# Weight quantization shared with ScalarE, the causal mask on GpSimd in every batch, and a new instruction order, in a one-core transformer layer

## The chip, the cores and the metric

The kernel runs on one core of a Trainium2 chip. Its metric is the device time of one execution, in microseconds (us); below it is the median over several runs. The engines are named as in the profile: PE (TensorE: matmuls and transposes, PEld its weight loads), DVE (VectorE), ACT (ScalarE), POOL (GpSimd) and SP (SyncE, which here only issues DMAs).

## The reference

Four batches of 512 tokens by 512 channels, float32. A layer has two halves, each preceded by the same kind of gate:

```
gate(x, s, w, u):  # per channel, scans over the tokens in both directions
    ek = exp(min(s, 30));  ekv = ek * s;  euk = exp(min(u + s, 30))
    num = scan_forward(ekv) + scan_backward(ekv) - ekv + euk * s
    den = scan_forward(ek)  + scan_backward(ek)  - ek  + euk
    return sigmoid(x) * num / max(den, 1e-8) * (0.8 + 0.2 * tf)
x = x + attention(gate(x, side, w1, u1))      # 16 heads of 32, causal softmax
h = gate(x, side, w2, u2)
x = x + q_act(silu(q_act(h) @ q_w(w_gate).T) * (q_act(h) @ q_w(w_up).T)) @ q_w(w_down).T
```

The last matrices are 2048 by 512 (gate, up) and 512 by 2048 (down). `q_w` and `q_act` quantize blocks of 32 values along the contracted axis: a block is divided by a power of two taken from its largest magnitude, each value is rounded half to even to a tiny float format and clipped (weights: one fraction bit, at most 6), and multiplied by the power of two again.

## The kernel before

Everything is planned at build time. The code first registers each small piece of work with `add(engine, cost, run, r, w, ...)`, which derives the dependences from the tiles read and written and numbers the operations. Then `Plan.follow` walks through `SEQUENCE`, a list of these numbers that a search found offline against the costs given to `add`, and the instructions are issued in that order; on each engine they run in exactly that order. The costs only serve this planning (PSUM banks are also assigned by it).

DVE instructions marked `shared=True` and POOL instructions are planned to take turns: a POOL instruction gets a dependence on the last shared DVE instruction ahead of it in the list, so it waits for it.

The stages, by batch `b`:

- **Gate** (`wkv_pieces`, lines 602 to 718). Per batch and block of 128 channels: the side input is loaded and transposed (L615), exponentials on ACT (L619 to L634), products on POOL (L626, L652, L654, L665), two forward and two backward scans on DVE (L640, L645) with a scaling on ACT between them (L650), a reciprocal by logarithm and exponential on ACT (L658, L659, L661), and the ratio on DVE (L666, L670, L672, L675). The first gate also transposes x (L689, L692), the second writes its result to DRAM (L709, L712).
- **Attention** (`Group`, four groups of four heads per batch). Projections (L765 for queries and keys, with ACT copies L776 and L779; L731 for values). `find_max`: scores by PE with a mask added by matmuls (L790, L794), row maxima on DVE (L804). `lay_max`: these maxima are split and transposed into `low` (ACT L816, DVE L817, PE L821, ACT L824). `weights`, the score turn: in three turns per group, scores by key (PE L848 subtracts the maxima, L855 adds the products), exponential on ACT (L862) into `pT`. `weigh`: `pT` times the values and times ones (L887, ACT L897). `finish`: the sums are spread and their reciprocals applied (L910, L915, L922, L926). The output projection is L983, its residual L989; the second gate's sigmoid L992 and product L993 follow.
- **Causal mask of the weights.** Two of the three score turns of a group hold diagonal blocks, two each. In batches 0 and 1 (`LATE = 2`) four matmuls (L844) write the mask into the PSUM tile `scores` before the products are added. In batches 2 and 3 two POOL selects (L867) set the upper part of the diagonal blocks of `pT` to zero after the exponential.
- **Weights of the second half** (`weight_piece`, `quantize_weight`). 24 pieces of 128 by 1024, each loaded by SP, quantized and transposed by DMA into `wgT`, `wuT` and `wdT`. They are registered with batch 0 and spread by the list over the first 478 us. Per piece: block maxima (L489), scale and its inverse (L492, L495), division (L513), clip (L515), exponent bits as 16-bit integers (L518), then a factor that turns them into a magic number (L521), all on DVE; POOL adds the magic number (L523), subtracts it (L524), and multiplies by the scale (L525).
- **Second half** (`inner_piece`, `down_piece`). Per tile of 128 tokens: gate and up matmuls (L1020), SiLU on ACT (L1027), product on DVE (L1030), quantization (DVE L489 to L537, POOL L544), DMA transpose, down matmuls (L1061), residual (L1074). Those of batch `b` run beside the attention of later batches. The very last tile is transposed by PE (L555, L1037).

ACT needs a table set loaded for exponential and logarithm, sigmoid, or SiLU. Operations that need one name it in `add`, and a load (L1145) is issued wherever the set changes in the list.

Of the kernel before, what the change touches and what calls it, by code (L numbers as in the profile page):

```python
# [24 lines left out]
ROUND_W, LEAST_W, LIMIT_W = 1.5 * 2.0**22, 0.25, 1.5  # L25
# [116 lines left out]
BEGIN = 3.0  # L142
# [6 lines left out]
0 1 183 30 6 919 27 245 196 33 31 28 2 3 4 29 9 32 34 45 39 40 66 184 185 186 5 187 11 188 16 35 12 10 189 13 14  # L149
41 7 67 937 72 78 42 43 68 46 73 17 47 8 44 15 197 79 105 106 198 50 18 199 19 23 51 74 80 48 49 81 82 111 112  # L150
55 56 107 113 117 36 37 52 190 246 89 20 21 22 38 191 53 54 83 57 58 62 192 94 144 69 118 70 90 95 87 24 25 26
88 119 91 145 120 121 96 200 71 146 59 150 75 84 85 60 86 92 122 93 61 133 201 202 128 97 76 213 108 160 151 277
152 129 156 109 126 127 134 110 77 98 99 203 63 64 101 100 130 193 65 247 114 131 132 115 123 147 161 278 116
279 280 281 248 135 102 194 195 402 262 157 148 124 149 137 125 138 103 104 139 136 204 282 249 250 290 285 140
214 168 164 205 215 217 216 286 291 283 206 218 207 208 343 153 141 142 143 263 264 287 265 221 158 165 169 162
166 170 159 163 167 171 219 292 220 284 222 174 172 173 175 223 226 260 261 227 288 289 266 228 224 225 403 230
404 180 344 231 345 181 182 209 346 405 239 251 240 267 210 241 211 229 347 232 242 406 349 350 243 176 348 293
233 234 351 294 212 408 352 252 268 235 356 353 410 295 244 177 296 357 258 259 236 297 407 253 354 237 360 355
254 275 276 303 309 466 154 155 467 592 238 304 358 269 298 411 305 306 307 361 362 299 359 363 364 365 412 310
255 311 415 308 300 301 468 409 322 323 470 270 366 369 477 469 367 475 416 413 478 370 371 476 428 178 179 419  # L160
420 398 414 471 271 272 479 429 430 482 483 421 431 480 481 312 417 418 484 399 337 486 422 338 257 256 302 324
368 472 473 474 339 432 423 424 340 487 425 488 426 485 489 400 535 313 533 433 536 447 490 314 491 537 540 534
401 541 538 449 273 274 544 450 372 427 586 920 539 587 715 448 493 492 494 542 341 342 325 495 588 589 496 590
545 326 327 543 546 497 591 498 464 465 595 547 315 597 598 548 549 602 599 328 716 512 513 593 550 553 551 596
603 552 709 584 600 554 555 329 594 717 613 614 316 330 604 615 606 616 582 607 601 605 609 653 608 658 583 610
317 527 654 528 651 652 585 529 617 611 659 655 530 531 612 373 532 660 618 632 633 318 656 662 657 710 663 664
711 712 713 319 661 714 718 671 665 672 331 332 333 374 375 720 634 673 719 674 675 721 676 666 725 722 667 767
649 689 668 726 635 690 736 727 772 737 738 763 703 723 724 728 732 334 669 729 730 768 731 773 785 765 766 733
734 769 770 776 786 735 376 764 825 321 320 385 670 819 771 787 788 704 650 820 777 821 823 822 336 335 377 386
434 963 705 378 387 830 706 774 789 790 803 824 775 831 778 826 827 707 804 846 828 379 847 779 708 780 781 832  # L170
835 380 848 849 850 829 851 817 782 783 836 818 964 864 865 878 381 833 839 840 841 435 837 388 891 389 834 838
892 884 879 965 880 842 382 843 844 845 390 391 392 906 436 437 881 886 438 887 907 885 893 888 904 905 393 394
395 784 957 384 383 451 396 397 499 882 916 908 439 889 890 894 452 453 917 918 883 951 952 440 441 454 953 958
933 455 909 954 934 959 895 896 897 960 961 921 442 443 444 955 935 500 968 922 456 898 457 458 962 501 899 900
973 969 956 984 924 925 926 927 910 459 936 966 967 974 911 460 928 929 985 1004 930 502 1005 446 445 923 461
970 931 971 1101 514 1143 938 990 462 463 932 556 986 1006 901 1007 987 902 1008 1009 939 988 1024 914 515 516
517 503 504 505 506 975 940 507 942 972 943 976 1025 1052 1028 1033 518 944 945 946 947 557 1029 989 977 915 978
979 1026 912 992 980 948 1054 1053 981 949 508 509 1085 1034 913 1027 982 1086 1030 983 1031 1035 993 558 559
1068 1087 1032 1036 1037 1038 1039 1088 1046 1047 1069 519 520 521 1040 1041 1042 1089 1090 903 941 1010 1095
991 950 511 510 569 522 1048 1096 1102 1097 1099 523 1091 1049 570 560 1106 1092 995 1103 1098 1107 524 996 1104  # L180
1137 1100 1012 1043 571 572 1138 1013 561 1108 1044 1105 1070 1139 1140 1050 1141 1109 1071 1115 1093 997 998
999 1000 1116 1117 1142 1001 562 563 1051 1111 1112 1002 1094 1122 1147 1123 1148 1224 526 525 1011 994 619 1045
1423 1014 1218 1003 1225 573 574 575 1113 1162 620 1157 1110 1114 564 1118 1175 1176 1177 1149 1155 1163 1015
1441 1016 1158 1226 1195 1119 576 1196 1120 1191 1192 1150 1197 1151 1198 1156 1152 1159 1199 1200 1153 1214
1017 1018 1019 1121 1154 1164 1215 565 577 1160 1161 1166 1219 1193 566 1165 1167 1168 1220 1221 1222 1251 1227
1223 578 1194 621 1229 1252 1253 1254 1230 1228 1169 1170 1171 1234 1231 1245 1172 1173 1235 622 1020 1236 623
1280 1285 1255 1256 1257 1216 1232 1238 1233 1237 1241 1424 1334 567 568 636 1174 1328 579 580 581 1239 1240
1258 1278 1246 1281 1279 1242 1243 1282 1217 1286 1272 1298 1283 1289 1290 1273 1244 637 638 1284 1329 1274 677
1469 1291 1330 1332 639 1287 1288 1299 1300 1021 1316 1331 1301 1317 624 625 626 1275 1302 1318 1337 1319 1338
1339 1292 1333 1470 1335 1340 627 628 1320 1321 1293 1341 1344 1326 1294 1295 1336 1276 1327 629 1342 1022 1343  # L190
1471 1345 1348 1296 1357 1346 1347 1351 1349 1358 1277 1359 1360 1361 640 1380 641 642 643 644 645 646 631 630
1297 1023 691 1463 648 647 739 1355 1350 1362 1376 1352 1353 1354 1378 1356 1379 1381 1410 1408 1377 1411 1409
678 679 680 681 1382 682 683 684 685 686 692 693 694 1385 695 696 697 1398 1386 1399 698 1420 1400 1421 1401 687
1383 1384 1422 740 1439 1455 1456 741 742 1387 1440 1389 1402 1403 699 1388 700 688 751 1464 1457 1437 743 1438
1412 1465 1467 1458 1390 1391 1459 1466 1472 1413 1460 1425 1392 744 745 746 1474 1393 752 1426 1490 1414 1394
1491 1475 1428 1510 1511 1512 1415 1513 1473 701 1468 747 1429 748 1461 749 753 1430 1431 754 1476 1479 1536
1492 1395 1514 1477 1493 1396 1480 1483 1484 1485 1515 1611 702 1427 791 792 1432 793 1481 1541 1443 1444 1442
1496 1397 750 1445 805 1462 1478 1482 1534 1494 1530 1542 1535 1537 1418 1486 755 1433 794 756 757 1434 758 1531
1560 1495 1419 1435 1532 1416 1533 759 1417 1487 1488 1489 1538 1561 1562 1539 1540 1576 795 1543 1577 1605 1436
1446 1593 1545 1447 1594 1448 1554 1595 1606 1555 1596 1544 1607 1608 1609 1556 1612 1597 1498 1598 1601 1449  # L200
1450 796 1451 1452 797 798 1557 806 1616 1499 1546 1614 1547 1617 1453 1610 1516 1497 1738 1518 1621 1548 1549
1550 760 761 1599 1600 799 1454 1500 762 1613 1501 1602 1618 1551 1622 1615 1647 1552 807 1648 1519 808 1623
1578 1649 1558 1650 1619 1579 1625 1651 1502 1620 1626 1624 1628 800 1943 852 1517 1553 1732 1674 1627 1675 1559
853 1669 1629 809 810 811 1630 1603 1652 1667 1670 1604 1657 1632 1739 1658 1740 1668 1687 1659 1660 801 1661
1631 1671 1689 1688 1676 1707 1708 854 855 856 1672 1673 1703 1633 1678 1662 1709 1733 1663 1710 1734 1735 1679
1677 1704 1736 857 812 858 1743 1711 1705 1680 1741 1712 1744 1681 1682 1683 813 1713 1737 1728 1684 1745 1706
1742 1746 1730 1664 1729 1748 1685 1752 1753 1765 1754 1731 1766 814 815 1714 1747 1796 1665 1767 1768 1749 1797
1666 1750 1769 1770 1759 1751 1771 1760 1794 1772 1520 802 1852 866 1686 1846 816 1503 867 1801 1802 1795 1055
1056 1755 859 1756 1757 1798 1758 1814 1853 1816 1057 1815 860 1799 1800 1773 1774 1847 1817 1854 1832 1848 1504
1833 868 1803 1818 1834 1788 1849 1850 1857 1835 1805 1806 1807 1836 1837 1858 861 1851 1804 1862 1808 1809 1810  # L210
# [43 lines left out]
def adaln_attn_ffn(  # L254
# [16 lines left out]
    nc = tc.nc  # L271
# [941 lines left out]
```

## Time and profile before

| | |
|---|---|
| time, median of 3 runs | 762.88 us (762.46 to 764.87) |
| profiled execution | 767.15 us, span 765.4 us |
| instructions | 14324 |
| mean granted PE clock | 0.971 of full |
| ACT table loads, L1145 | 74, 1.283 us each |
| DMA | 68.57 MB, mean 90 GB/s |

The span reaches from the first to the last instruction; the rest of the execution lies around it. In the profile a group of instructions is a line of the kernel with engine, operation, tiles and shape; its columns are the total busy time in us, the mean of one in ns, and the idle time of the engine just before them with what ended it. A "stretch" gives busy us of each engine between two times, with the number of instructions in brackets, then the granted PE clock, the share of DMA and GB/s.

### The profile page before, as it was taken

How to read it: one execution, taken by the hardware profiler on the slowest of the kernel's cores; microseconds unless marked ns; L12 is line 12 of the kernel's file. 1: busy time of each engine (PE TensorE's matmuls, PEld its weight loads, DVE VectorE, ACT ScalarE, POOL GpSimd, SP SyncE). 2: the span in 40 equal slices, each digit the busy share in tenths (PEclk: the TensorE clock that was granted, in tenths of full speed). 3: DMA queues.
4: the chain of work that ended last, by engine and by line, in shares of the span. 5: the costliest groups of instructions: out<-in, count | busy, mean ns of one | idle time of the engine just before them, and what ended most of it. 6: DMA issues, size and time to landing. Idle time of an engine off the chain costs nothing.

```text
span 765.4 us, 14324 instructions
## 1 busy us (share of the span) xinstructions
PE 679.4 (89%) x5636; PEld 356.0 (47%) x5666; DVE 639.3 (84%) x881; ACT 485.1 (63%) x687; POOL 428.0 (56%) x316
## 2 busy tenths in 40 slices
PE   3578889877999988599998869999999999999995
PEld 2344445444444554354554444544444455444442
DVE  5888899998999999999999987766565669789996
ACT  5998798769466878636688877634541566433421
POOL 1976683867778587778686875332231223334440
PEclk9688999989999999999999999999999999999999
DMA  7553152131345523325343100233313225446542
GB/s 220 152 138 82 30 132 63 43 98 41 83 125 127 148 53 98 86 72 138 90 118 112 42 16 8 69 63 76 97 36 84 56 42 100 100 94 164 103 104 82
DMA packets 115730, 68.57 MB, mean 90 GB/s; under 512 B 71632, under 2 KB 98256, under 8 KB 115664
## 3 DMA queue, kind: packets, MB, share of 16 engines
q1 hardware_dynamic: 115664, 67.67, 34.9%
q8 instruction: 44, 0.72, 0.4%
q14 instruction: 22, 0.18, 0.1%
HBM read 38.81 MB, written 12.58 MB: 67 GB/s over the span
## 4 chain that ended last, share of the span: by engine, by line
PE 65%; DVE 16%; ACT 10%; issue 4%; DMA 3%; POOL 2%; SPq 0%; DVEq 0%; POOLq 0%; ACTq 0%
PE bank L1020 13%; PE bank L765 11%; PE bank L983 7%; PE bank L887 7%; PE bank L731 6%; PE bank L1061 6%; PE scores L794 4%; PE scores L855 3%; DVE aside L804 3%; DVE f L645 2%; ACT pT L862 2%; ACT L1145 2%; DVE aside L489 2%; DVE r L640 2%; PE scores L790 2%
## 5 line engine op out<-in xcount | busy, mean ns | idle before, releaser
L804 DVE TENSOR_REDUCE aside<-scores 128x4 f32<-128x1536 f32 (+2 forms) x64 | 95.8, 1496 | 24.6 <-PE scores L794 21.7
L544 POOL TENSOR_TENSOR y<-q,ysc 128x1024 bf16<-128x1024 fp8e4 x30 | 57.3, 1909 | 99.8 <-DVE q L537 68.4
L765 PE MATMUL bank<-y1T,wqkvT 128*128 128x512 f32 x240 | 112.7, 615 | 0.4 <-DVE y1T L675 0.4
L652 POOL TENSOR_TENSOR f<-f,eu 128x512 f32<-128x512 f32 x56 | 71.3, 1272 | 52.2 <-DVE f L645 34.2
L1145 ACT ACT_TABLE_LOAD x74 | 94.9, 1283 | 1.3
L1027 ACT ACTIVATE y<-bank 128x512 f32<-128x512 f32 x64 | 38.1, 597 | 83.7 <-PE bank L1020 65.5
L489 DVE TENSOR_REDUCE aside<-y 128x32 f32<-128x1024 f32 (+1 forms) x74 | 79.9, 1080 | 8.5 <-POOL y L993 4.9
L862 ACT ACTIVATE pT<-scores 128x1536 f32<-128x1536 f32 (+1 forms) x48 | 76.3, 1590 | 15.6 <-PE scores L855 11.6
L1020 PEld LDWEIGHTS <-y2qT 128*128 128x128 bf16 x512 | 48.4, 98 | 65.0 <-issue 12.5
L645 DVE TENSOR_TENSOR_SCAN f<-aside,r 128x512 f32<-128x512 f32 x56 | 71.2, 1275 | 7.1 <-ACT r L650 4.7
L765 PEld LDWEIGHTS bank<-y1T,wqkvT 128*128 128x128 f32 x240 | 45.3, 196 | 51.5 <-issue 49.0
L1030 DVE TENSOR_TENSOR y<-y,bank 128x512 f32<-128x512 f32 x64 | 42.9, 681 | 29.5 <-PE bank L1020 15.0
L1020 PE MATMUL bank<-wuT,y2qT 128*128 128x512 bf16 x255 | 65.6, 379 | 0.2
L1020 PE MATMUL bank<-wgT,y2qT 128*128 128x512 bf16 x231 | 63.6, 380 | 1.6 <-issue 0.5
L523 POOL TENSOR_TENSOR y<-y,qT 128x1024 f32<-128x1024 f32 x24 | 51.2, 2132 | 20.1 <-DVE qT L521 17.7
L1061 PE MATMUL bank<-wdT,qT 128*128 128x512 bf16 x252 | 57.8, 379 | 1.0 <-ACT qT L1037 0.7
L983 PE MATMUL bank<-woT,attnT 128*128 128x512 f32 x128 | 58.3, 598 | 0.0
L887 PE MATMUL bank<-pT,v 128*32 128x256 f32 (+1 forms) x768 | 54.2, 355 | 0.8 <-ACT ld L692 0.4
L887 PE MATMUL bank<-pT,ones 128*32 128x256 f32 (+1 forms) x768 | 53.0, 348 | 0.0
L731 PE MATMUL bank<-wqkvT,y1T 128*128 128x512 f32 x112 | 51.6, 603 | 0.5 <-DVE attnT L926 0.5
L524 POOL TENSOR_TENSOR qT<-y,qT 128x1024 bf16<-128x1024 f32 x24 | 51.2, 2133 | 1.5 <-DVE maxima L817 0.7
L535 DVE TENSOR_TENSOR y<-y,aside 128x1024 f32<-128x1024 f32 (+1 forms) x50 | 50.1, 1003 | 1.1
(145 smaller groups left out, 1360.6 us busy)
## 6 DMA issues: line engine op xcount, KB each, us to landing
ld<-in_fside_BxSxS_dram SPq DMA_DIRECT2D x20, 256.0 KB, 3.0
y<-in_L_ffn_w_gate_dram SPq DMA_DIRECT2D x8, 512.0 KB, 4.5
ld<-in_x_dram SPq DMA_DIRECT2D x16, 256.0 KB, 3.1
xa<-in_x_dram SPq DMA_DIRECT2D x16, 256.0 KB, 2.9
r<-ld SPq DMA_DIRECT2D x16, 256.0 KB, 2.6
rl<-r SPq DMA_DIRECT2D x16, 256.0 KB, 3.1
y<-in_L_ffn_w_up_dram SPq DMA_DIRECT2D x8, 512.0 KB, 3.9
x<-xa SPq DMA_DIRECT2D x16, 256.0 KB, 2.3
```

What stands on the lines that cost most here:

```text
L489: add(DVE, reduced(width), lambda: nc.vector.tensor_reduce(am, y.rearrange("p (g e) -> p g e", e=BLOCK), AX.X, ALU.max, apply_absolute_val ...
L645: nc.vector.tensor_tensor_scan(f[:, ::-1], d.to_broadcast([P, T]), r[:, T - 1 :: -1], r[:, T:], ALU.mult, ALU.add)
L652: add(POOL, pooled(512), lambda f=f: nc.gpsimd.tensor_tensor(f, f, eu, ALU.add), r=[keu], w=[kf])
L731: nc.tensor.matmul(bank[banks.at[0]], src[:, c, ts(t, P)], wqkvT[:, c, 2 * C :], start=c == 0, stop=c == NC - 1)
L765: nc.tensor.matmul(bank[banks.at[0]], wqkvT[:, c, s * C + g * P : s * C + (g + 1) * P], src[:, c, :], start=c == 0, stop=c == NC - 1,)
L804: add(DVE, reduced(HG * (i + 1) * P), lambda i=i: nc.vector.tensor_reduce(found[:, i, :], scores[:, :, offset[i] : offset[i] + (i + 1) * P ...
L862: add(ACT, 0.18 + 0.82e-3 * HG * offset, lambda: nc.scalar.activation(pT[:, :, :offset], scores[:, :, :offset], AF.Exp), r=["scores"], w=[ ...
L887: nc.tensor.matmul(heads[j * D : (j + 1) * D, which, q0 : q0 + width], lhs, pT[:, j, o : o + width], start=k == 0 and which == 0, stop=k = ...
L983: nc.tensor.matmul(bank[banks.at[0]], attnT[:, g, ts(t, P)], woT[:, g, :], start=g == 0, stop=g == NG - 1)
L1020: nc.tensor.matmul(bank[dst], src[:, c, :], w[:, c, ts(ic, 512)], start=c == 0, stop=c == NC - 1)
L1061: nc.tensor.matmul(bank[banks.at[0]], qT[b, t, k // 8][0][:, k % 8, :], wdT[:, k, :], start=k == 0, stop=k == NI // P - 1,)
L1145: nc.scalar.preload_act_table_set(SETS[table])
```

## The change

Three things change.

- In `quantize_weight` the clip and the bit mask on DVE go. ACT computes the magic number from the magnitude, |y| times `ROUND_W`, rounded to bfloat16; DVE applies a lower bound; POOL adds and subtracts as before; the clip is done on DVE on the rounded bfloat16 values, between POOL's subtraction and its multiplication. A piece has ten operations besides its DMAs before and after.
- The mask matmuls of `weights` go, and POOL's selects are used in all batches: 32 more selects, 64 matmuls fewer. The list has 2489 numbers instead of 2457.
- `SEQUENCE` is another list, and some planning costs differ (`BEGIN`, scans, POOL operations, the select). Read against the calls of `add`, the new list changes ACT's table set 66 times, the old one 74. Up to the second pair of gate and up matmuls (L1020; each tile of 128 tokens has four pairs) the new list holds every compute operation that the old one holds there, the 32 selects, and 14 more.

```diff
-ROUND_W, LEAST_W, LIMIT_W = 1.5 * 2.0**22, 0.25, 1.5
+ROUND_W, LEAST_W, LIMIT_W = 1.0625 * 2.0**22, 0.25, 1.5
...
-BEGIN = 3.0
+BEGIN = 6.5
...
 SEQUENCE = """
...
 """
...
-    LATE = 2
...
         add(DVE, tt(width) + 0.06, lambda: nc.vector.tensor_tensor(blocks(y), blocks(y), inv, ALU.mult),
             r=[ki], w=ky)
-        add(DVE, ts2(width), lambda: nc.vector.tensor_scalar(y, y, LIMIT_W, -LIMIT_W, ALU.min, ALU.max),
-            w=ky, shared=True)
-
-        add(DVE, ts2(width), lambda: nc.vector.tensor_scalar(
-            mg.bitcast(I16), y.bitcast(I16)[:, 1::2], EXP_BITS >> 16, None, ALU.bitwise_and
-        ), r=ky, w=[kmg], shared=True)
-        add(DVE, 0.16 + 0.26e-3 * width, lambda: nc.vector.tensor_scalar(mg, mg, LEAST_W, ROUND_W, ALU.max, ALU.mult),
+        add(ACT, acted(width), lambda: nc.scalar.activation(mg, y, AF.Abs, scale=ROUND_W), r=ky, w=[kmg])
+        add(DVE, 0.16 + 0.27e-3 * width, lambda: nc.vector.tensor_scalar(mg, mg, LEAST_W * ROUND_W, None, ALU.max),
             w=[kmg], shared=True)
-        add(POOL, 2.3, lambda: nc.gpsimd.tensor_tensor(y, y, mg, ALU.add), r=[kmg], w=ky)
-        add(POOL, 1.95, lambda: nc.gpsimd.tensor_tensor(mg, y, mg, ALU.subtract), r=ky, w=[kmg])
+        add(POOL, 2.13, lambda: nc.gpsimd.tensor_tensor(y, y, mg, ALU.add), r=[kmg], w=ky)
+        add(POOL, 2.13, lambda: nc.gpsimd.tensor_tensor(mg, y, mg, ALU.subtract), r=ky, w=[kmg])
+        add(DVE, 0.16 + 0.27e-3 * width, lambda: nc.vector.tensor_scalar(
+            mg, mg, LIMIT_W, -LIMIT_W, ALU.min, ALU.max
+        ), w=[kmg], shared=True)
         add(POOL, 1.9, lambda: nc.gpsimd.tensor_tensor(blocks(q), blocks(mg), sc, ALU.mult), r=[kmg, ks], w=ky)
...
-            masked = d0 and self.b < LATE
-
             def turn():
-                for j in range(HG if masked else 0):
-                    nc.tensor.matmul(diagonal(j, d0), mask16, many(ident16, d0), start=True, stop=False, skip_group_check=True)
...
-            for o in d0 if not masked else ():
+            for o in d0:
                 block = pT[:, :, o : o + P]
-                add(POOL, 1.1, lambda block=block: nc.gpsimd.affine_select(
+                add(POOL, 0.65, lambda block=block: nc.gpsimd.affine_select(
```

## The prediction

> **What bounds the kernel now.** I read part 1 of the page first, then the slices of part 2, then the busy times of two stretches, cut where the second pair of gate and up matmuls (L1020) begins: 459.80 us in the timeline; one early pair runs at 434 us, and from the second on they run steadily.
>
> ```profile
> PE 679.4 (89%) x5636; PEld 356.0 (47%) x5666; DVE 639.3 (84%) x881; ACT 485.1 (63%) x687; POOL 428.0 (56%) x316
> ```
> ```profile
> PE   3578889877999988599998869999999999999995
> ...
> PEclk9688999989999999999999999999999999999999
> ```
> ```profile
> 0.00:460.00 460.00, 384.55 (x3594) 212.53 (x3597) 414.50 (x529) 348.65 (x516) 328.62 (x243) 0.95 0.36 96
> 460.00:766.00 306.00, 294.84 (x2043) 143.42 (x2069) 224.82 (x353) 136.48 (x172) 99.40 (x73) 1.00 0.35 80
> ```
>
> The columns of the stretches are PE, PEld, DVE, ACT, POOL. The whole-span share says "PE-bound"; the stretches say it is two kernels. After 460 us PE works 294.8 of 306 us: nothing but less PE work shortens that. Before 460 us PE lacks 75.4 us, DVE only 45.5 us (27 of them in the first 100 us), and nobody is full alone. A finer cut of that part:
>
> ```profile
> 80.00:200.00 120.00, 99.38 (x1109) 56.53 (x1107) 110.58 (x132) 97.06 (x142) 82.05 (x54) 0.96 0.26 71
> 200.00:260.00 60.00, 59.86 (x440) 30.50 (x439) 55.05 (x77) 38.86 (x57) 45.45 (x29) 1.00 0.42 110
> 260.00:340.00 80.00, 65.64 (x798) 38.04 (x797) 75.73 (x98) 57.87 (x83) 57.24 (x37) 0.98 0.37 97
> 340.00:400.00 60.00, 59.42 (x424) 29.68 (x426) 56.29 (x78) 40.13 (x59) 46.87 (x35) 1.00 0.41 107
> 400.00:460.00 60.00, 48.76 (x648) 28.35 (x643) 55.10 (x68) 49.36 (x73) 45.99 (x36) 0.97 0.22 57
> ```
>
> The softmax stages (80 to 200, 260 to 340, 400 to 460) have PE at 81 to 83% and DVE at 92 to 95%; the projection stages between have PE at 99% and DVE still at 92 to 94%. So DVE is the tightest engine of the first 460 us, with PE alternately beside it. The weights are quantized there: 23 of 24 clips (L515) start before 460 us, about evenly spread.
>
> **The change, part by part.** The rows:
>
> ```profile
> L523 POOL TENSOR_TENSOR y<-y,qT 128x1024 f32<-128x1024 f32 x24 | 51.2, 2132 | 20.1 <-DVE qT L521 17.7 <-DVE qT L518 2.4
> L867 POOL TENSOR_SCALAR_AFFINE_SELECT pT<-pT 128x512 f32<-128x512 f32 x32 | 19.9, 634 | 29.3 <-DVE q L537 18.1 <-ACT pT L862 11.1
> L515 DVE TENSOR_SCALAR y<-y 128x1024 f32<-128x1024 f32 x24 | 18.9, 786 | 0.2
> L518 DVE TENSOR_SCALAR qT<-y 128x1024 int16<-128x1024 int16 x24 | 16.5, 689 | 0.4
> L521 DVE TENSOR_SCALAR qT<-qT 128x1024 bf16<-128x1024 bf16 x24 | 10.5, 436 | 0.4
> L844 PE MATMUL scores<-ident,mask 128*128 128x256 bf16 x64 | 10.1, 281 | 7.1 <-ACT pT L862 4.8 <-DVE aside L804 2.2
> ```
>
> *DVE, weights.* Out go L515, L518 and L521: 18.9 + 16.5 + 10.5 = 45.9 us. In come, per piece, a max and a clip over 1024 bf16 elements. Neither is in the trace; L521 has their size and type, 0.436 us each, so 48 x 0.436 = 20.9 us. Net **-25.0 us** of DVE, 23/24 of it, -24.0, before the cut. The ends: L521's shortest, 0.401 us, and L515's median for f32, 0.684 us, which would put 48 x 0.25 = 12 us back.
>
> *ACT, weights.* 24 Abs over 1024 elements from SBUF. Nearest: sigmoid from SBUF, 512 elements, 0.630 us (L992); each element more costs (1.874 - 1.448)/512 = 0.83 ns (L862's two sizes), so 0.630 + 0.426 = 1.06 us. A 512-element PSUM copy at 0.58 gives 1.01 as lower end, an activation with a bias at 0.72 gives 1.15 as upper: 24 to 28 us, I take +25.4. The new order changes the table set 66 times instead of 74; L1145 costs 1.283 us, so -10.3. Net **+15 us** of ACT, which had 111 us free before 460. Abs is given no set of its own; Relu and Copy (L619, L622) run in the trace without a load.
>
> The Trainium skill, "ScalarE: Activation LUTs", section "Table sets: the hidden batching unit", says the cheap functions, abs among them, are in every set; no Abs is in this trace. By the section "Rules for kernel authors" of the same page, max, min and the like belong on VectorE, up to about 3 times faster there: that speaks against this edit. By that rule the sum would be a loss of some 9 us, not a gain.
>
> The trace's own rows: 0.69 us of DVE are bought with 1.06 us of ACT, 24 x 0.37 = 9 us dearer; a loss if both were equally full, but before 460 us ACT has 111 us free and DVE 45.5.
>
> *POOL, weights.* Add, subtract and scale stay (2.13, 2.13, 1.91). But the clip now stands between subtract and scale, so POOL hands over to DVE and back once more per piece. This wait is not in the trace. L523 waits 20.1/24 = 0.84 us on average for the same kind of handover today, so 0 to 20 us of POOL idling; the three shared DVE operations per piece (1.9 us, beside which the planned turns keep POOL still) shrink to two (0.87 us), 24 us in the other direction. I take zero for the sum. Queued behind a waiting scale are POOL's f and eu products, which feed ACT's L658 and DVE's L675; if POOL idled the full 20 us on the path, the gain from DVE would be gone.
>
> *Mask.* Out: 64 matmuls L844, **-10.1 us** of PE, with 7.1 us of waiting before them that the next matmul (L848) inherits. In: 32 selects at 0.634 = **+20.3 us** of POOL, all before 340 us in the old order. Batches 2 and 3 already do this, and there the list of waits has L887, which reads the masked tile, waiting for POOL 0.8 us in all.
>
> *Order.* No instruction but those above is added, and no DMA. Read against the old list, up to the cut (the second pair of gate and up matmuls) the new one holds every compute operation of the old one, the 32 selects, and 14 more. On PE: 3 projections (L765 112.7/30 = 3.76 each) and a score turn (L848 and L855, 73.7/48 = 1.54): 12.8 us. On DVE: a backward scan (1.27) and a clip (L537, 0.42): 1.7 us. On ACT 6.6 us, on POOL 1.0 us; three of the eight table loads saved lie there, 3.8 us.
>
> **The sum**, against the profiled execution (span 765.4). Two ways to carry the idle time over:
>
> DVE keeps its 45.5 us of idling: the cut comes at 414.5 + 1.7 - 24.0 + 45.5 = 437.7. What follows took 765.4 - 459.8 = 305.6 us, PE-bound, and loses 12.8 of PE work: 292.8. Span 730.5, **-34.9**. PE would then idle 437.7 - (384.6 - 10.1 + 12.8) = 50.4 us before the cut, 25 less than now.
>
> PE keeps its idling, and only the masks go: **-10.1**, span 755.3.
>
> The truth should lie between. First, 7 of the 24 pieces lie in the stretches where PE is at 99% (L513: 4.86 + 3.65 of 29.0 us); a lighter DVE shortens nothing there, which takes 0.29 of the 24.8 us between the two sums: -27.7 is left. Second, the neighbours get fuller. ACT rises from 349 to 348.7 + 24.3 - 3.8 + 6.6 = 375.8 busy us, 76% to 86% of the time to the cut, POOL from 329 to 350, 71% to 80%. Between 80 and 460 us PE waits for ACT 22.1 us today (for L862 9.8 + 4.8, L897 3.1, L824 3.0, L659 1.4, by the list of waits). With ACT's free share going from 24% to 14% these may stay or double, 0 to 22 us; I take 9.7, a little under the middle, since the new list can put Abs where ACT is idle. **-18.0**.
>
> Span 747.4; that execution took 767.15, 1.75 around its span, so 749.1. The median of the runs is 762.88, 4.3 below it: 762.9 - 18.0 = **744.9 us**.
>
> **Rivals.**
>
> *A. The waits only change hands* (PE's idling stays). For: PE is named as waiting for ACT's exp, L804 and L817, no weight operation. Against: DVE is at 92 to 95% while PE waits, and L804 and L817 queue behind the weight work. 762.9 - 10.1 = 753.
>
> *B. DVE was the whole bound before 460.* For: 92 to 95% in all five stretches. Against: the two PE-full stretches. 762.9 - 34.9 = 728.
>
> *C. Slower: the select's turn in POOL's queue.* Place: the second key pair of each group in batches 0 and 1 (8 turns), where weighing follows the score turn directly. Price: two selects, 1.27 us, behind one 2.13 us operation, 3.4 us on PE per turn, 27 us in all: 762.9 - 18.0 + 27.2 = 772. It decides from 18.0/8 = 2.3 us per turn. For: in the row above, selects and POOL wait for each other's neighbours (18.1 us behind L537), and POOL is 71% full. Against: batches 2 and 3 show 0.8 us.
>
> *D. No change, or the edit is not what it says*: if each Abs brought a table load and one back, 48 x 1.283 = 62 us more on ACT, over half of its 111 us free before 460, and with the 25 us of Abs most of it; some 772 if 10 of them landed on the path. Relu and Copy without a load speak against it.
>
> **How the numbers follow.** Forecast (738 to 750) 0.50, A (750 to 758) 0.20, B (728 to 738) 0.13, C 0.11, D and others 0.06, half of it near no change. A measurement of this kernel can tell about 0.3%, 2.3 us. Faster 0.83, same 0.04, slower 0.13. The range leaves out the lower half of B, C and D; upward it takes in A with the dearer end of the bf16 operations on DVE if 9 of those 12 us reach the end (753 + 9): 732 to 762.
>
> **What would show it.** Right: DVE busy near 614, PE 669, ACT 500, POOL 448; 66 rows of L1145; Abs near 1.06 us and the bf16 clip near 0.44; the second pair of gate and up matmuls between 440 and 458 us, then about 293 us of full PE. Wrong: PE's idling before that point still 75 us (A); L887 or its weight load waiting for POOL for over 16 us (C); a clip at 0.69 us; more table loads than 66.

## The result, and the profile after

The changed kernel takes **758.28 us** (median of 20 runs, 756.64 to 763.76); the kernel before, run beside it, 764.5 us (20 runs, 762.3 to 766.88). The ratio is 0.9923 [0.991, 0.9936]: 6.2 us less, where 18.0 were forecast. The profiled pair stands a little wider apart, 765.4 us of span before and 755.6 after, since that execution of before lies 2.6 us above its median and that of after 1.0 below.

In this section line numbers are those of the kernel after: the Abs is L516, the lower bound on DVE L517, POOL's add L519, subtract L520, the new clip L521, POOL's scale L524; the matmuls that PE does for a row maximum L789 and L793 (before L790, L794), DVE's row maximum L803 (L804), the score turn L843 and L850 (L848, L855), the exp L857 (L862), the select L862 (L867), the weighing L882 (L887), gate and up L1015 (L1020). In the experiments they shift by up to seven.

Part 1 of the page of after, and two rows of its slices:

```profile
PE 673.1 (89%) x5602; PEld 353.2 (47%) x5602; DVE 617.8 (82%) x857; ACT 496.5 (66%) x703; POOL 447.1 (59%) x348
...
PE   1568798976999988899999779999999999999996
...
PEclk9999899997999999999999999999999999999999
```

DVE fell by 21.5 us, POOL rose by 19.1, ACT by 11.4, PE fell by 6.3. Now the two stretches, cut where the second pair of gate and up matmuls begins. It begins at 460.66 us, in the kernel before at 459.80:

```profile
0.00:460.66 460.66, 387.07 (x3578) 214.53 (x3579) 396.90 (x511) 373.02 (x544) 350.82 (x279) 0.97 0.36 97
460.66:756.00 295.34, 286.00 (x2025) 138.64 (x2023) 220.85 (x346) 123.45 (x159) 96.29 (x70) 1.00 0.33 81
```

The reader is to see that the cut did not move, although DVE (third number after the comma) has 17.6 us less to do before it, 396.9 for 414.5. Its idling there went from 45.5 to 63.8 us. PE's idling hardly changed: 460.66 - 387.07 = 73.6 us, before 75.4. PE's busy time before the cut is 384.6 - 10.1 + 12.8 = 387.3 by the prediction's terms and 387.07 by the trace, so the masks' matmuls are gone and the moved projections are there. What was won lies behind the cut: from there to the end 294.9 us instead of 305.6, since work that stood there now stands ahead of it. The finer cut:

```profile
80.00:200.00 120.00, 100.01 (x1095) 57.24 (x1094) 108.27 (x127) 103.28 (x155) 92.81 (x72) 0.93 0.26 71
200.00:260.00 60.00, 59.77 (x424) 30.48 (x420) 54.47 (x78) 44.35 (x65) 48.10 (x35) 1.00 0.44 124
260.00:340.00 80.00, 69.24 (x860) 39.89 (x860) 72.67 (x95) 65.01 (x93) 63.67 (x50) 1.00 0.31 82
340.00:400.00 60.00, 59.84 (x451) 29.78 (x450) 54.30 (x75) 45.67 (x64) 49.30 (x37) 1.00 0.47 122
400.00:460.00 60.00, 49.79 (x572) 28.48 (x571) 50.98 (x64) 51.73 (x72) 45.06 (x35) 0.97 0.22 57
```

In the softmax stretches PE is still at 83 to 87%, DVE at 85 to 91% instead of 92 to 95%. And four rows, the sizes of the change:

```profile
L1140 ACT ACT_TABLE_LOAD x66 | 84.7, 1283 | 1.2
...
L862 POOL TENSOR_SCALAR_AFFINE_SELECT pT<-pT 128x512 f32<-128x512 f32 x64 | 39.6, 635 | 50.8 <-DVE q L536 25.1
...
L524 POOL TENSOR_TENSOR y<-qT,wsc 128x1024 bf16<-128x1024 bf16 x24 | 45.9, 1911 | 19.3 <-DVE qT L521 12.2
L519 POOL TENSOR_TENSOR y<-y,qT 128x1024 f32<-128x1024 f32 x24 | 51.2, 2134 | 6.1 <-DVE qT L517 3.9
```

Every piece costs what was forecast: Abs 1.05 us (25.1 in all), L517 and L521 0.466 and 0.418 us, 66 table loads. POOL's two waits in a piece, 19.3 and 6.1 us, sum to 25.4 us, and in the kernel before to 25.3 (20.1 before the add, 5.2 before the scale): they changed places. The sizes were right; what they are worth was wrong.

### The profile page after: what moved, and what is told of

Its sections match the earlier page's. It is cut to its first block, busy times and chain, and to the rows that moved or that the text cites. A ratio compares the mean times of both kernels' runs of the same rounds, so it can differ in the third digit from the quotient of the medians.

```text
span 755.6 us, 14257 instructions
## 1 busy us (share of the span) xinstructions
PE 673.1 (89%) x5602; PEld 353.2 (47%) x5602; DVE 617.8 (82%) x857; ACT 496.5 (66%) x703; POOL 447.1 (59%) x348
## 4 chain that ended last, share of the span: by engine, by line
PE 70%; DVE 12%; ACT 7%; POOL 3%; DMA 3%; issue 2%; SPq 1%; DVEq 0%; POOLq 0%; ACTq 0%
PE bank L1015 14%; PE bank L764 12%; PE bank L882 7%; PE bank L978 7%; PE bank L1056 7%; PE bank L730 7%; DVE aside L803 5%; PE scores L793 4%; PE scores L850 4%; ACT pT L857 3%; DVE f L644 2%; PE scores L789 2%; PE scores L843 2%; PE bank L910 1%; DMA ld<-in_L_attn_w_qkv_dram 1%
## 5 line engine op out<-in xcount | busy, mean ns | idle before, releaser
L803 DVE TENSOR_REDUCE aside<-scores 128x4 f32<-128x1536 f32 (+2 forms) x64 | 95.8, 1498 | 32.1 <-PE scores L793 29.3
L764 PE MATMUL bank<-y1T,wqkvT 128*128 128x512 f32 x240 | 110.8, 607 | 0.1
L857 ACT ACTIVATE pT<-scores 128x1536 f32<-128x1536 f32 (+1 forms) x48 | 76.3, 1589 | 16.5 <-PE scores L850 16.1
L1015 PEld LDWEIGHTS <-y2qT 128*128 128x128 bf16 x512 | 48.6, 98 | 64.5 <-issue 11.3
L862 POOL TENSOR_SCALAR_AFFINE_SELECT pT<-pT 128x512 f32<-128x512 f32 x64 | 39.6, 635 | 50.8 <-DVE q L536 25.1
L1015 PE MATMUL bank<-wgT,y2qT 128*128 128x512 bf16 x256 | 65.9, 380 | 0.0
L1015 PE MATMUL bank<-wuT,y2qT 128*128 128x512 bf16 x256 | 65.7, 379 | 0.0
L524 POOL TENSOR_TENSOR y<-qT,wsc 128x1024 bf16<-128x1024 bf16 x24 | 45.9, 1911 | 19.3 <-DVE qT L521 12.2
L519 POOL TENSOR_TENSOR y<-y,qT 128x1024 f32<-128x1024 f32 x24 | 51.2, 2134 | 6.1 <-DVE qT L517 3.9
L882 PE MATMUL bank<-pT,v 128*32 128x256 f32 (+1 forms) x768 | 53.9, 353 | 0.8 <-ACT kT L621 0.4
L882 PE MATMUL bank<-pT,ones 128*32 128x256 f32 (+1 forms) x768 | 53.2, 349 | 0.0
L520 POOL TENSOR_TENSOR qT<-y,qT 128x1024 bf16<-128x1024 f32 x24 | 51.2, 2134 | 1.3
```

The source lines that it names most:

```text
L764: nc.tensor.matmul(bank[banks.at[0]], wqkvT[:, c, s * C + g * P : s * C + (g + 1) * P], src[:, c, :], start=c == 0, stop=c == NC - 1,)
L803: add(DVE, reduced(HG * (i + 1) * P), lambda i=i: nc.vector.tensor_reduce(found[:, i, :], scores[:, :, offset[i] : offset[i] + (i + 1) * P ...
L857: add(ACT, 0.18 + 0.82e-3 * HG * offset, lambda: nc.scalar.activation(pT[:, :, :offset], scores[:, :, :offset], AF.Exp), r=["scores"], w=[ ...
L882: nc.tensor.matmul(heads[j * D : (j + 1) * D, which, q0 : q0 + width], lhs, pT[:, j, o : o + width], start=k == 0 and which == 0, stop=k = ...
L1015: nc.tensor.matmul(bank[dst], src[:, c, :], w[:, c, ts(ic, 512)], start=c == 0, stop=c == NC - 1)
```

## The experiments

**Theory 1, "turns"**, formed from these views: the time up to the cut is PE's busy time plus an idle time that belongs to the order, namely PE's waits for the first loads and for the short hand-offs of attention; DVE's freed time becomes idling. **Rivals**: DVE is still the bound; POOL's handover in the clip eats what DVE gave; before the cut no engine is the bound, and an operation costs what it adds to the chains of work that wait for each other, some part of its time (called "chains" below, and "half price" once two runs had suggested about half); or the gain is the new list's alone.

### The start

After has five loads ahead of the first side load, and PE's first transpose starts at 13.24 us instead of 6.76. The first experiment puts that one load at the head of the list.

```diff
 SEQUENCE = """
-6 183 196 30 953 0 247 27 935 1 28
+0 6 183 196 30 953 247 27 935 1 28
...
```

> The changed kernel, but the first load of the side input (L607) is issued ahead of the five loads that the new order puts in front of it; nothing else moves. In the changed kernel PE's first transpose of it starts at 13.24 us, before the change at 6.76. Theory (chains): before the second gate and up pair no single engine is the bound, DVE's saving was never on the path, and a late start is partly caught up by slack: 0 to 3 us faster than the changed kernel, 755 to 758. Rival (DVE bound, gain lost again): DVE's saving was made and given back, 6.5 us of it here: 5 to 7 us faster, near 752.

Measured: 758.08 us, 0.992 [0.9899, 0.994]; no difference from after. In the first 80 us PE's waits for side loads fall from 12.2 to 5.9 us and those for the loads of the projection weights rise from 9.6 to 15.9: together 21.8 in both. The late load cost nothing that another load does not cost instead, and no DVE bound came out (near 752).

### Undoing one edit

Masks on PE again (32 selects out, 64 matmuls in, other operations in their places):

```diff
+    LATE = 2
...
+            masked = d0 and self.b < LATE
...
+                for j in range(HG if masked else 0):
+                    nc.tensor.matmul(diagonal(j, d0), mask16, many(ident16, d0), start=True, stop=False, skip_group_check=True)
...
-            for o in d0:
+            for o in d0 if not masked else ():
```

> The changed kernel with the mask of batches 0 and 1 by matmuls again and its 32 selects dropped; order and quantization as changed. PE +10 us, POOL -20. Theory (chains): the mask matmuls stand in the score chain and on PE, so most of 10 us comes back: 763 to 768. Rival (DVE bound, PE idles anyway, POOL and ACT too full): 0, or a few us faster than the changed kernel: 753 to 759.

Measured: 763.08 us, 0.9987 [0.9972, 1.0002], 4.8 above after. Weights as before, in the new list with only the pieces' own operations placed anew:

```diff
-        add(ACT, acted(width), lambda: nc.scalar.activation(mg, y, AF.Abs, scale=ROUND_W), r=ky, w=[kmg])
...
+        add(DVE, ts2(width), lambda: nc.vector.tensor_scalar(y, y, LIMIT_W, -LIMIT_W, ALU.min, ALU.max),
+            w=ky, shared=True)
...
```

> The changed kernel and its order with the old weight quantization (clip, bits and factor on DVE, no Abs); only the operations of the quantization and the DMA transposes behind them are placed anew in the list. DVE +25 us, ACT -25. Theory (chains): DVE's load is not what ends the wait, under a third of it comes back: 758 to 766. Rival (DVE bound): most of 25 us comes back: 773 to 783.

Measured: 771.28 us, 1.0101 [1.0082, 1.0121]. Both edits in the old list:

```diff
 SEQUENCE = """
-6 183 196 30 953 0 247 27 935 1 28
+0 1 183 30 6 935 27 247 196 33 31 28
...
```

> Both edits in the order of before; only the edited operations, the transposes behind them and the selects are placed anew. Theory (chains): the edits lengthen the chains of weights and masks (one more handover each), and without a new order that costs: 765 to 780. Rival (the resources decide, the order little): like the changed kernel or better, 750 to 760.

Measured: 780.62 us, 1.0213 [1.019, 1.0235]. The first run is at the low end of "chains"; the second fits neither side (758 to 766, 773 to 783); the third lies just past the upper end of "chains" (765 to 780). The first two look like half price: 4.8 us for 10 of PE, 13.0 for 25 of DVE. But old weights in the new list, and new operations in the old list, are both slower than the kernel before. So an edit undone in a list that was made for it also pays for the misfit of operations and list, and its worth can't be read from it. That the 13.0 us are misfit and not the price of more DVE work is argued: no run adds DVE work and keeps the list. The next runs only leave out or double, and keep the list.

### Leaving out and doubling, list kept

```diff
-        add(DVE, tt(width) + 0.06, lambda: nc.vector.tensor_tensor(blocks(y), blocks(y), inv, ALU.mult),
-            r=[ki], w=ky)
         add(ACT, acted(width), lambda: nc.scalar.activation(mg, y, AF.Abs, scale=ROUND_W), r=ky, w=[kmg])
```

> Left out: the division of every weight piece by its block factors (L514, 24 x 1.21 us = 29.0 us of DVE), so the quantized weights are not the reference's; everything else keeps its order. Theory 'turns' (before the cut the order runs in turns of PE and ACT, DVE is not what ends last, so its freed time becomes idling): 755 to 760 us, within 0.3% of the changed kernel. Rival 'half price' (every engine's microsecond before the cut is worth about half, as the two undone edits showed): 742 to 748. Rival 'DVE is the bound before the cut': 729 to 735.

```diff
-        add(DVE, 0.16 + 0.27e-3 * width, lambda: nc.vector.tensor_scalar(
-            mg, mg, LIMIT_W, -LIMIT_W, ALU.min, ALU.max
-        ), w=[kmg], shared=True)
```

> Left out: the clip on the 16 bits (L521, 24 x 0.42 = 10.0 us of DVE, and with it POOL's handover to DVE and back between its subtract and its scale), so weights above the limit are not the reference's. Theory 'turns': 754 to 759. Rival 'half price': 750 to 754. Rival 'POOL's handover eats what DVE gives' (L524 waits 19.3 us for the clip): 738 to 748, and POOL's wait before the scale gone in the trace.

```diff
-            for o in d0:
+            for o in d0 if self.b > 1 else ():
```

> Left out: the 32 selects of batches 0 and 1 (20.3 us of POOL), with nothing in their place, so these two batches attend to later keys too. Theory 'turns': 754 to 759. Rival 'half price': 746 to 751. Rival 'POOL's queue is the bound': 737 to 742. Together with the kernel whose masks went back to PE (763.1) it says what 32 selects cost and what 64 mask matmuls cost.

```diff
         add(ACT, acted(width), lambda: nc.scalar.activation(mg, y, AF.Abs, scale=ROUND_W), r=ky, w=[kmg])
+        add(ACT, acted(width), lambda: nc.scalar.activation(mg, y, AF.Abs, scale=ROUND_W), r=ky, w=[kmg])
```

> Each Abs is done twice into the same tile: 24 x 1.05 = 25.1 us more of ACT, 23 of them before the cut, nothing else changed and nothing left out. Theory 'turns' (ACT is in the turns, and the second Abs stands ahead of exps and copies that PE waits for): 768 to 783. Rival 'half price': 768 to 773. Rival 'ACT has room' (87 us idle before the cut): 757 to 763.

| what | busy time | median us | ratio to before | against after |
|---|---|---|---|---|
| after | | 758.28 | 0.9923 [0.991, 0.9936] | |
| no division | DVE -25.1 | 759.2 | 0.9928 [0.9914, 0.9943] | +0.9 |
| no clip | DVE -7.9 | 756.04 | 0.9896 [0.988, 0.9911] | -2.2 |
| no select | POOL -18.6 | 756.13 | 0.9902 [0.9884, 0.9919] | -2.2 |
| Abs twice | ACT +24.0 | 761.16 | 0.9961 [0.9947, 0.9976] | +2.9 |

Taking 25 us from DVE gives nothing. The clip with its handover is worth some 2 us, the selects the same, and 24 us more of ACT cost 3. The first three came as "turns" expected. Of the clip's rival only the sign came: POOL's wait before the scale fell from 19.3 to 6.4 us, and the time hardly followed. The doubled Abs went against "turns" (768 to 783) and came as "ACT has room" expected: PE waits for exps, but more work on ACT made those waits hardly longer (12.4 us instead of 11.4 in the longest group). The list of waits says why DVE's 25 us gave nothing; first after, then the kernel without the division, PE's longest waits up to 460 us (total, times, longest):

```profile
PE bank L614 <- DMA ld<-in_fside_BxSxS_dram: 12.4, 4, 9.6
PE scores L789 <- ACT pT L857: 11.4, 11, 1.6
PE bank L474 <- DMA ld<-in_L_attn_w_qkv_dram: 9.6, 5, 3.0
PE scores L789 <- DVE aside L803: 6.3, 4, 1.7
PE bank L820 <- DVE maxima L816: 6.1, 7, 1.9
PE scores L843 <- DVE aside L803: 4.4, 4, 2.0
PE scores L843 <- ACT pT L857: 4.1, 5, 1.2
```
```profile
PE scores L783 <- ACT pT L851: 11.4, 11, 1.6
PE bank L608 <- DMA ld<-in_fside_BxSxS_dram: 11.2, 3, 8.6
PE bank L470 <- DMA ld<-in_L_attn_w_qkv_dram: 10.6, 5, 3.5
PE bank L814 <- DVE maxima L810: 6.4, 7, 1.9
PE scores L783 <- DVE aside L797: 6.2, 4, 1.6
PE scores L837 <- ACT pT L851: 4.1, 5, 1.2
PE scores L837 <- DVE aside L797: 4.0, 3, 2.0
```

Wait by wait they are the same, to 0.4 us apart from the loads. PE waits for loads, for the exp of the turn before, for the row maximum and for its remainder (L816); no operation that quantizes weights is among them, and none of these hand-offs got shorter by more than 0.4 us when DVE had 25 us less.

### The same in the kernel before

Was DVE the bound there, as the forecast said? The old kernel and list, without the division:

> The kernel before, its order kept, with the division of every weight piece left out (L514, 24 x 1.21 us = 29.0 us of DVE, somewhat more than the change takes from DVE), so its quantized weights are not the reference's. My prediction's step 'DVE is the tightest engine of the first 460 us' wants 18 to 35 us less: 729 to 746. Rival 'turns' (PE's idling before 460 us comes from its turns with ACT and from the start, and DVE's 92 to 95% are no bound): within 0.4% of before, 760 to 766 where before is 763 to 764.

Measured: 766.9 us, 1.0028 [1.0006, 1.0049]. Part 1 of its page, and the stretch up to 460 us:

```profile
PE 682.7 (89%) x5636; PEld 357.7 (47%) x5666; DVE 617.7 (81%) x857; ACT 485.5 (63%) x687; POOL 428.0 (56%) x316
```
```profile
0.00:460.00 460.00, 387.01 (x3585) 213.82 (x3590) 394.35 (x506) 348.74 (x515) 328.56 (x243) 0.94 0.36 96
```

There is 20.1 us less of DVE before 460 us (394.4 for 414.5), and the kernel is not faster. PE's idling over the span is 83.5 us instead of 86.0. The step is refuted in the kernel that it was about. Then the old kernel without the mask of batches 0 and 1:

```diff
-            masked = d0 and self.b < LATE
+            masked = False
...
-            for o in d0 if not masked else ():
+            for o in d0 if self.b >= LATE else ():
```

> The kernel before, its order kept, with the mask of batches 0 and 1 left out: the 64 matmuls L844 (10.1 us of PE) go and no select takes their place, so these batches attend to later keys too. Theory 'turns' (PE's own work is what the end follows): 8 to 12 us less, 752 to 756 where before is 763 to 764. Rival 'the waits of 7.1 us before these matmuls stay, and PE idles for the rest' : 759 to 764.

Measured: 765.74 us, 1.003 [1.0002, 1.0058]; not faster either, though 10.1 us of PE are gone. That is neither what "turns" expected nor wholly the rival (759 to 764): PE's idling did not grow (84.5 us for 86.0). Part 1 of its page, and its stretches from 0 to 80, 80 to 200 and 260 to 340 us (the masks stood between 80 and 340):

```profile
PE 678.7 (89%) x5572; PEld 355.0 (47%) x5602; DVE 639.2 (84%) x881; ACT 485.5 (64%) x687; POOL 428.4 (56%) x316
```
```profile
0.00:80.00 80.00, 53.55 (x212) 30.52 (x216) 62.94 (x83) 66.13 (x106) 51.82 (x54) 0.96 0.51 142
80.00:200.00 120.00, 97.77 (x1074) 55.24 (x1070) 109.99 (x131) 96.43 (x142) 81.38 (x54) 0.93 0.28 71
...
260.00:340.00 80.00, 66.20 (x779) 38.09 (x777) 76.09 (x101) 56.73 (x81) 58.17 (x38) 0.91 0.34 94
```

With 64 matmuls fewer PE is as busy as before (678.7, 679.4), and the granted clock (third number from the end) is 0.93 and 0.91 where it was 0.96 and 0.98. That is 120 x 0.03 + 80 x 0.07 = 9.2 us of full clock, an estimate of what PE lost there, and from 80 to 340 us its busy time fell by 1.1 us (from 224.9 to 223.7) instead of 10.1. The group of score matmuls that changed most there, first before, then without masks:

```profile
L794 PE MATMUL scores<-qk 32*128 32x512 f32 x64 | 9.1, 640 | 0.0
```
```profile
L791 PE MATMUL scores<-qk 32*128 32x512 f32 x64 | 12.0, 825 | 0.0
```

Each takes 825 ns instead of 640, 2.9 of the 9 us that came back; the other large groups changed by less than 5%. This is one execution of each kernel. Over its whole span the mean clock is 0.971 in both, because the kernel before has its low clock at the start, where PE waits for loads and is busy 51.5 of 80 us:

```profile
0.00:80.00 80.00, 51.49 (x191) 29.42 (x192) 61.75 (x81) 65.38 (x104) 51.01 (x53) 0.83 0.50 142
```

Over all runs of the two kernels side by side the mean granted clock was 0.962 without masks (12 runs) and 0.976 before (23 runs). That difference can't be turned into time as it stands: at the same mean of 0.971 the two runs without masks took 764.70 and 764.96 us and the four of before 761.83 to 763.34, so equal means do not bring the 10 us back. Nor does it belong to the masks alone: the same list without the division had 0.969 (12 runs). So it is shown, in one execution of each, that the clock was lower where the masks had stood and that matmuls there became longer; that the missing masks made it so is not shown (the new list without its 32 selects keeps 0.978, after has 0.980). The Trainium skill, "TensorE: Matmul & The Clock Gate", section "HAM oscillation — how this bites in real kernels", asks that PE have no idle gaps of more than about 3.4 us, since the clock is halved after them. Here the trace differs: in the kernel before the granted clock is 0.50 from 25 to 41 us, and no wait of PE in the whole run is longer than 3.1 us. No run here isolates what brings the half clock.

### A positive control

So far all runs say what does not count. If PE waits for the row maximum, 25 us taken from that should count:

```diff
-                    found[:, i, :], scores[:, :, offset[i] : offset[i] + (i + 1) * P], AX.X, ALU.max, negate=True
+                    found[:, i, :], scores[:, :, offset[i] : offset[i] + (P if i == 3 else (i + 1) * P)], AX.X, ALU.max, negate=True
```

> The changed kernel, order kept; the largest of the four row maxima (L803, 2048 elements, 16 times, 2.30 us each) looks at the first 128 keys of each head alone (512 elements, 0.70 us by the row of that size), so the softmax subtracts a maximum over part of the keys. It takes 16 x 1.6 = 25.7 us from DVE, as much as the weights' edit did, some 19 of it before 460 us, but in the turn: PE's next score turn and the exps wait for it. Theory 'turns': 5 to 18 us less than the changed kernel, 740 to 753. Rival 'no microsecond of DVE pays before the cut': 755 to 760.

Measured: 755.38 us (six runs, 750.56 to 759.93), 0.9885 [0.9846, 0.9925]. Inconclusive: three runs took 750.56 to 752.70, as "turns" has it, three 758.05 to 759.93, as the rival has it, and none lies near the median. In the profiled execution, one of the faster three, DVE has 16.1 us less to do before 460 us (380.8 for 396.9), and PE's waits for L803 are what they were, 6.3 and 4.4 us, and its idling did not fall (85.3 us for 82.5); the 4.6 us of span come from PE's busy time, 665.7 for 673.1 (29 matmul records are missing in it). The shortened maxima were not those that PE waits for. That PE's idling falls when a hand-off gets shorter is therefore argued from the list of waits, not shown.

### The list by itself

The last question is whether the new list made the gain. Four lists were searched anew with equal effort, by moving one operation at a time in a model of the queues with the trace's durations: for the old operations (starting from the old list), for each edit alone and for both (starting from the new one). The edits are those of the diffs above; the list begins, for the old operations:

```diff
 SEQUENCE = """
-0 1 183 30 6 919 27 245 196 33 31 28
+0 27 1 2 4 183 3 28 9 11 33 39
...
```

> None of the two edits: all operations of the kernel before, in an order searched anew for them. Theory 'the gain is the search's, not the operations'' : faster than before, 750 to 759 where before is 764. Rival 'the operations pay, and the old order was already as good as theirs can be': 761 to 767.

> The weights' edit alone (masks of batches 0 and 1 as matmuls on PE), in an order searched for these operations. Theory 'the search's gain': within 0.5% of the run with none of the edits. Rival 'DVE pays once the order fits': 6 us or more below that run (of 24 us taken from DVE before the cut).

> The masks' edit alone (the weights as in the kernel before), in an order searched for these operations. Theory 'the search's gain': within 0.5% of the run with none of the edits. Rival 'PE's 10.1 us pay once the order fits': 5 to 10 us below that run.

> Both edits, with the order of the changed kernel searched on from, with the engines' and the first loads' starts taken from its trace. Theory 'the search's gain': 745 to 756, and within 0.8% of the run with none of the edits. Rival 'the operations pay': 10 us or more below the run with none of the edits.

Against expectation masks alone came out at the time of before, which looked like luck of the search. So three were searched a second time, with another seed or from another start:

> All operations of the kernel before, a second search of equal effort with another seed (the first gave 752.4). If the search's luck is small: 749 to 756. If it is as large as the differences between the four orders: anywhere from 745 to 764, and then the worth of the edits can't be read from single orders.

> Both edits, a second search of equal effort with another seed (the first gave 744.8). If the search's luck is small: 741 to 748. If large: 745 to 758. If 'both' stays below 'none' in this pair too, the operations carry part of it.

> The masks' edit alone, searched with equal effort from the order found for the old operations, selects put in behind their exps (the first, from another start, gave 763.8). If PE's 10.1 us pay once the order fits: 741 to 748. If they come back as a slower clock or as waits: 750 to 757. If the search's luck rules: 757 to 766.

| operations | first search | second search |
|---|---|---|
| old | 752.36, 0.9854 [0.9829, 0.9879] | 757.65, 0.9922 [0.9893, 0.995] |
| weights edited | 752.83, 0.985 [0.9825, 0.9875] | |
| masks edited | 763.76, 0.9989 [0.9972, 1.0006] | 753.48, 0.9869 [0.9845, 0.9892] |
| both edited | 744.84, 0.9751 [0.9723, 0.9778] | 752.48, 0.9855 [0.9832, 0.9878] |

The old operations with another list (and after's planning costs) are 11.7 and 6.3 us faster than before: as fast as the changed kernel, or faster. Two searches for the same operations differ by 5.3, 10.3 and 7.6 us, as much as the whole change. Both edits stand 7.5 and 5.2 us below none in either pair, which speaks for some worth of theirs; with two lists each, it is not settled how much. The first pair lies between the two expectations (within 0.8%, or 10 us or more). Weights alone came within 0.5 us of none, as "the search's gain" expected. Nor is it on record that the two starting lists, the old and the new, had been searched equally long before. Part 1 of the first lists for old operations and for both:

```profile
PE 678.1 (90%) x5634; PEld 357.1 (47%) x5666; DVE 635.1 (84%) x881; ACT 481.9 (64%) x685; POOL 428.2 (57%) x316
```
```profile
PE 671.1 (90%) x5572; PEld 352.7 (47%) x5602; DVE 616.0 (83%) x857; ACT 492.4 (66%) x701; POOL 446.7 (60%) x348
```

With their spans, 754.6 and 745.6 us, PE's idling is 76.5 and 74.5 us. In the kernel before and the two runs that leave its operations out it was 83.5 to 86.0, in after and the five runs that leave out, shorten or double there 81.7 to 85.3 (some 30 matmul records that miss in part of the traces may make some 2 us of such a difference, an estimate). Over the seven searched lists it goes from 71.5 to 84.5. So with the list kept it stays, whatever the other engines lose or gain by leaving out or doubling, and it moves with the list. Where operations were exchanged for others it moved too: with the masks put back into after's list it is 78.3, perhaps since the mask matmuls fill some of it; with the old weights there it is 91.3, and with both edits in the old list 96.5. What varies with the list kept is PE's busy time: for the same 5602 matmuls it is 673.1 us in after and 669.0 to 678.3 in the four runs that leave out or double there. So one profiled execution says little about the differences of 2 or 3 us in the table above; those rest on the medians. The list for both edits at 744.84 us is the fastest kernel of this study, 13.4 us below the changed one. It is the forecast's number by chance, not by its mechanism: DVE idles 54 us up to 460 us there, not 45.5.

## Why the prediction was wrong

- **"DVE is the tightest engine of the first 460 us"** is the step that failed. 92 to 95% busy was read as a bound. Leaving out DVE work made neither kernel faster (25 us in after: +0.9 us; 20 us before the cut in the kernel before: +2.7). Most of PE's idling up to the cut in after is waits for loads (26 us), exps (15.5), row maxima (10.7) and their remainder (6.1). Rival A had the sign of it, that no weight operation is among PE's waits, and it was weighed too lightly; its mark came, PE's idling before the cut is 73.6 us where it named 75. One reading beside the step was wrong as well: of DVE's 45.5 us of idling 21.7 lie in the first 100 us, not 27.
- **The choice between the two sums** hung on it: the two lie 24.8 us apart, and 17.6 of them were given to the one in which DVE keeps its idling (-27.7, from which 9.7 were taken back for ACT). DVE's idling grew by 18.3 us. The sum in which PE keeps its idling gave -10.1 of span; the profiled pair shows -9.8, the medians -6.2.
- **That sum came nearest, but not for its reason alone.** It takes PE's 10.1 us of masks for a gain wherever they stand. In the old list the same 10.1 us were worth nothing (in the profiled execution PE was at a lower clock where they had stood); in the new one going back to matmuls costs 4.8 us, misfit included. And the old operations gain 6.3 to 11.7 us from a list alone, a term that the prediction did not have: it counted what the new list moves across the cut (12.8 us of PE, as measured) and let idle time follow the engines, not the list. So it is luck in part that -10.1 lies so near the profiled pair.
- **Sizes** held: 21.2 us for DVE's two new operations (20.9), 25.1 for Abs (25.4), 66 loads, selects 0.635 us, POOL's waits zero in sum. DVE's total fell by 21.5 us instead of 25.0 and PE's by 6.3 instead of 10.1; of the latter 2.3 us lie in a row of L1020 that has 231 records before and 256 after. The ACT waits taken as 9.7 us dearer did not come: PE's waits for L857 went from 14.6 to 15.5 us, and doubling Abs cost 2.9 us; to take 9.7 us off for ACT was a second error, of the opposite sign.
- **Rival C** did not come: the weighing or its weight loads wait 2.2 us in all for POOL. **Rival D** did not: no load more, and the faster time is measured.
- **The rule quoted from the skill** (max, min and the like belong on VectorE, by which the prediction had a loss of 9 us) prices both engines as if full. Here neither price applied: 25 us of DVE were worth nothing, 24 us of ACT 2.9, and weights edited against none, one searched list each, 0.5 us.

Open: how the worth of some 5 to 8 us that both edits show is shared between them, and whether more searches would leave it standing; what exactly in a list sets PE's idling, and so how much of the 6.2 us is the list's and how much the edits'. That PE's idling falls when a hand-off that PE waits for gets shorter was not shown.

## What to carry to other kernels

An engine at 95% beside one at 82% is no proof of a bound: look at what the engine that ends last waits for, and leave an operation out with the order kept, before its time is counted as gain. Where the order is a searched list, the order is a part of the change of its own: compare lists found with equal effort, at least two of each, or the luck of the search is taken for the worth of the edit. An edit undone in a list made for it measures the misfit too.

## What was not expected of the hardware

Less PE work can give no less PE time. Without 64 short matmuls (10.1 us) PE's busy time was 678.7 us instead of 679.4 in the profiled executions, with the granted clock at 0.93 and 0.91 instead of 0.96 and 0.98 in the stretches where they had stood, and one group of score matmuls at 825 ns instead of 640. Whether the clock fell because they were gone is not shown.
